# Row sums of image B's attention by transfer, and a reordered front, in a conv-attention kernel

## The chip, the cores and the metric

One core of one Trainium2 chip runs the whole program. The metric is the device time in microseconds (us) of one execution; less is better. PE is the matrix engine, PEld its weight loads, DVE the vector engine, ACT the scalar engine, POOL the GpSimd engine. SP is the engine that here only issues transfers. All data are fp32.

## The reference

The input is eight images of 512 channels and 32x32 pixels. Each is group-normed and sent through a block whose output is added back to the input:

```python
t = cbs(x, cv1_w, cv1_bn, 0)              # 1x1 conv, batch norm, SiLU
ys = [t[:, :C], t[:, C:]]                 # C = 256
for i in range(2):
    yi = ys[-1]
    z = cbs(yi, m_cv1_w[i], m_cv1_bn[i], 1)               # 3x3 conv
    z = bot_attention(z, m_qkv_w[i], m_rw[i], m_rh[i])    # 4 heads of 64, 1024 pixels
    z = silu(bn(conv2d(z, m_cv2_w[i], 0)))
    ys.append(yi + z)
return cbs(concatenate(ys), cv2_w, cv2_bn, 0)
```

Attention divides by the row sums of the exponentials. They are the subject of the larger part of the change.

## The kernel before

**Staging.** A front (roughly the first 77 us) norms the first images, turns the 3x3 filters into transformed filters (`make_u`) and begins the first 1x1 convolutions (`cv1`). Then the loop over p = 0 to 3 takes a pair of images A = 2p and B = 2p + 1. For each of two blocks (n = 0 and 1) it runs a transformed 3x3 convolution over both images (`conv3x3`), then per image a projection to q, k and v, the attention (`attention_fast`) and a 1x1 convolution (`m2`). Work of the next pair (its norm and its `cv1`, called `nxt`) is threaded in between. For p = 1 and 2 `nxt` is a Strassen scheme (`strassen_cv1`, seven products of four matmuls). For p = 0 it is direct, eight matmuls per output chunk. For p = 3 there is no next pair and the gap is filled with halves of the last convolution (`cv2_part`).

**Order.** Each engine executes its instructions in order. The order on each engine follows the program text, adjusted by a scheduler when the kernel is built. `tc.issue_after(x)` puts what its block traces on x's engine behind x on that engine.

**Attention.** Four groups (channel half c, pixel half) of eight key chunks. PE makes logits (line 1032), ACT the exponentials (line 1036), DVE adds them up into `acc` (lines 1050 and 1052), and PE multiplies by v (line 1066). The av product leaves PSUM at lines 1073 and 1074. The reciprocals of the row sums reach the output z by two ways:

- By transfer, for all groups but one: `sums` (line 1076) sums over partitions with four matmuls of 256 columns, ACT copies, SP stores the row to DRAM, `spread` (line 1122) reads it back as 128x8, inverts it on DVE (line 1126), writes it out and reads it back broadcast over 64 partitions each (line 1130). `scale` (line 1138) multiplies z by it. That is four transfers in sequence.
- At once (`at_once=True`), for the last group of image A in block 0 of p = 0 and of image B in block 0 of every p: `last_sums` (line 1093) makes the sums with an all-ones matrix of 64 columns, so that they already stand on all partitions. ACT copies them (line 1107), DVE adds the two halves (line 1182), inverts the full 128x512 (line 1183) and scales. Five further transfers (lines 1109 and 1114) and one add (line 1115) only keep the sums for a later range check.

**Behind image B's attention in block 0** (lines 2074 to 2096). PE runs the row sums, then `nxt.begin` (or the first `cv2_part`), then `m2` of image B, then the rest of `nxt`, then the next `conv3x3`. DVE makes the input tiles of that convolution: `tiles_in(Y2[0], ..., [0])` for image A, which has been ready for long, and `tiles_in(Y2[1], ...)` for image B, which needs all of m2's output. Each index i of `tiles_steps` has five pieces, from `w_ba`, `w_ec` or `w_g` (lines 554 to 561) to `v_in` (lines 595 to 603). Parts for image A with i = 1 and 2 come from DRAM (line 2084). In `conv3x3` PE writes `c_ps` (line 648), ACT copies a part (`c_m`, line 653), and DVE does the inverse transform (`c_t`, line 667, to z, line 699). PSUM has three buffers of this size.

**Front.** `make_u` treats one chunk (n, oc, k) in three steps i = 2, 0, 1. DVE does sums and differences (lines 430 to 435), ACT two copies per step (u0 and u5, lines 428 and 429), POOL the stores. Steps 0 and 1 first overwrite `mid` (lines 409 to 417). `chunk` is (0, 1, 0), `other` is (0, 1, 1). `behind_u` (line 1613) is called by `group_norm_part` while it applies the second image's norm on ACT (line 782) and puts work between these parts.

Of the kernel before, what the change touches and what calls it, by code (L numbers as in the profile page):

```python
# [47 lines left out]
ALU = mybir.AluOpType  # L48
# [13 lines left out]
def kernel(  # L62
# [325 lines left out]

    halves_of_u, copied_u, copies_behind, chunk_made = [], [None], [None], [None]

# [8 lines left out]

    def make_u(n, oc, k, area, full=None, new=u_new_late, stores=None, summed=True):  # L400

# [3 lines left out]
        for i in (2, 0, 1):  # L405
# [19 lines left out]
            if i < 2:  # L425
                yield last
            with tc.issue_after(copies_behind[0].ins) if copies_behind[0] else nullcontext():
                nc.scalar.activation(u0, c0, AF.Identity, scale=0.25)
                copied_u[0] = nc.scalar.copy(u5, c2)
            tt(u2, c0, c2, ALU.add)  # L430
            tt(u1, u2, c1, ALU.add)
            yield tt(u2, u2, c1, ALU.subtract)
            stt(u4, c2, 4.0, c0, ALU.mult, ALU.add)
# [52 lines left out]
    def stages(act, small, ps_big, ps_av, n_pt):  # L486
# [9 lines left out]
        silu_in, last_product, silued, last_exp, m2_silu, conv_product, cleared = [], [None], [None], [None], [None], [None], [None]  # L496
        shift_made, applied_x, projected = [None], [None], [None]

# [510 lines left out]
        def attention_fast(qkv, ao, at, behind, at_once=False):  # L1009
# [112 lines left out]
            def spread(g, s_dram):  # L1122

                rs = act.tile([P, HALF], F32, tag="rs", name="rs", bufs=4)
                rc = small.tile([P, QP], F32, tag="rc", name="rc", bufs=2)
                nc.vector.reciprocal(rc, total(g, s_dram))
                r_dram = tc.dram_tile([2, HALF], F32, name=f"r_dram{at + g}")
                nc.sync.dma_start(r_dram.rearrange("h (i r) -> (h i) r", r=QP), rc)
                for hd in range(2):
                    nc.sync.dma_start(  # L1130
                        rs[hd * HD : (hd + 1) * HD, :], r_dram[hd : hd + 1, :].to_broadcast([HD, HALF])
                    )
                return rs
# [33 lines left out]
            if not at_once:  # L1167
                with tc.issue_after(evicted[0].ins):
                    scale(g - 1, rss.pop(g - 1))
                return SimpleNamespace(  # L1170
                    evicted=evicted[0],
                    sums=lambda: s_drams.update({g: sums(g)}),
                    spread=lambda: rss.update({g: spread(g, s_drams[g])}),
                    scale=lambda: scale(g, rss.pop(g)),
                )
# [73 lines left out]

        def cv1(w_of, xts, y0s, y1, ocs, begun={}):  # L1250

            for oc in ocs:
                ps, at = begun.get(oc, (None, 0))
                ps = cv1_products(w_of, xts, oc, range(at, NX), ps)
                for half in range(NH):
                    dst = y0s[half][:, oc, :] if oc < NM else inner(y1, oc - NM, half)
                    silu(planes(dst), natural(ps[:, half, :]), bn_cv1 + oc)
# [114 lines left out]
        def strassen_cv1(w, xts, y0s, y1, t_tile):  # L1372
# [5 lines left out]

            def product(w, rhs, ps=None):
                onto = ps is not None  # L1380
                if not onto:
                    ps = ps_big.tile([P, 2, HALF], F32, tag="big", name="x_ps")
                for o in range(2):
                    for c in range(2):
                        nc.tensor.matmul(  # L1385
                            ps[:, o, :], w[:, c, ts(o, P)], rhs[c], start=(c == 0 and not onto), stop=(c == 1),
                            skip_group_check=onto,
                        )
                return ps
# [12 lines left out]
            y0_2, y1_1, y1_2 = y0s[1], side(y1, 0), side(y1, 1)  # L1402

            def begin():
                kept["ps"] = product(w["11"], b11)
                kept["m1"] = to(spare("p3"), kept["ps"])

# [5 lines left out]

            def sums(after=None):
                kept["t"] = t1, t2, t3, t4 = [t_tile() for _ in range(4)]
                for c in range(2):
                    tt(t1[:, c], b12[c], b11[c], ALU.subtract)
                with tc.issue_after(after.ins) if after else nullcontext():
                    for c in range(2):
                        tt(t2[:, c], b22[c], t1[:, c], ALU.subtract)  # L1420
                        tt(t3[:, c], b22[c], b12[c], ALU.subtract)
                        tt(t4[:, c], t2[:, c], b21[c], ALU.subtract)

# [24 lines left out]

            return begin, go_on, sums, rest, add_y0, add_y1, finish

        def cv2_part(w_of, rhs_of, oc, tag):

            ps = cv2_products(w_of, rhs_of, oc, range(2 * NM), ends=(0, 2 * NM - 1))
            part = act.tile([P, HW], F32, tag=tag, name="part")
            for half in range(NH):
                nc.scalar.copy(part[:, ts(half, HALF)], ps[:, half, :])
            return part
# [155 lines left out]
    def behind_u(c):  # L1613
        if c == 2:
            copies_behind[0] = s.applied_x[0]
            with tc.issue_after(s.added_eps[0].ins):
                next(chunk)
            with tc.issue_after(s.shift_made[0].ins):
                chunk_made[0] = next(chunk)
            with tc.issue_after(s.applied_x[0].ins), tc.issue_after(copied_u[0].ins):  # L1620
                s.cv1(w1_of, xs, y0s, Y1[0], Y_ORDER[2:3], begun)
            return s.silued[0]
        return copied_u[0] if c == 1 else s.silued[0] if c else None

# [63 lines left out]
    chunk = make_u(0, 1, 0, areas[0, 1, 0], new=u_new_early, stores=kept_back)  # L1688
    other = make_u(0, 1, 1, areas[0, 1, 1], new=u_new_early, stores=kept_back)
    with tc.issue_after(made.ins):  # L1690
# [9 lines left out]
    with tc.issue_after(copied_u[0].ins):  # L1700
        s.cv1(w1_of, xs, y0s, Y1[0], Y_ORDER[1:2], begun)
    first = begin(Y_ORDER[3], [0, 1])
    with tc.issue_after(made.ins), tc.issue_after(first.ins):
# [4 lines left out]
    with tc.issue_after(made.ins), tc.issue_after(s.silued[0].ins), tc.issue_after(first.ins):  # L1708
        multiplied, read, applied, powered = next(norm)
    copies_behind[0] = None  # L1710
    with tc.issue_after(powered.ins):
        put_stores(kept_back)
    with tc.issue_after(chunk_made[0].ins), tc.issue_after(powered.ins):
        for made in other:
            put_stores(kept_back)
# [84 lines left out]
    for p in range(NP):  # L1800
# [23 lines left out]
        def next_cv1(which, xts, y1, b):  # L1824
# [17 lines left out]
            if direct:  # L1842
                one = lambda oc: s.cv1(w_of, xts, y0s, y1, [oc])
                return SimpleNamespace(
                    begin=lambda: one(0), go_on=lambda: one(1), sums=nothing,
                    rest=lambda i: one(i) if i > 1 else None, adds=nothing, adds2=nothing, finish=nothing,
                    keep=lambda: keep_y(b, y0s, y1),
                )
            f = s.strassen_cv1(take_blocks("sw", None, which, SW_NAMES), xts, y0s, y1, t_qk)
            names = ("begin", "go_on", "sums", "rest", "adds", "adds2", "finish")  # L1850
            return SimpleNamespace(keep=lambda: keep_y(b, y0s, y1), **dict(zip(names, f)))
# [202 lines left out]
        def step_part():  # L2054
            next(parts_at, None)

        at_keys = ((1, 3), (2, 1), (2, 3), 3, (3, 2)) if more else [(g, at) if at else g for g in range(NG) for at in range(1, 4)]
        behind = hooks(NORM_B, {0: 1, 1: 1, 4: 1}, {key: step_part for key in at_keys}) | {
            NG + 1: begin_cv1(1, Y1[1], ia + 3)
        }  # L2060
        if not more:
# [10 lines left out]

            behind[NG + 1] = parts_of([0])
        end = s.attention_fast(qkv, z[:, :, 1], at_of(ib, 0), behind, at_once=True)
        while step_u():
            pass
        for _ in parts_at:
            pass
        if more:
            nxt.sums(end.scaled)  # L2080
        vs = v_units()
        for i in range(1, NI):
            for cp in range(3):
                nc.sync.dma_start(vs[i, cp][:, :, 0], v_dram[i][cp])
        with tc.issue_after(end.scaled.ins):
            s.tiles_in(Y2[0], putter(vs, 0), [0])
        last = s.m2(0, z[:, :, 1], Y1[1], lambda oc, half: inner(Y2[1], oc, half))
        if more:
            nxt.go_on()
            for i in range(4):  # L2090
                nxt.rest(i)
        else:
            parts_of([1, 2, 3])()
        with tc.issue_after(last.ins):
            s.tiles_in(Y2[1], putter(vs, 1))
            end.check()


        feed(units(1) + sqs(1, 0))
        z = new_z()  # L2100
# [214 lines left out]
```

## Time and profile before

| | |
|---|---|
| runs | median 2258.35 us of 3 (2257.54 to 2260.1) |
| the profiled execution | 2258.25 us, span of its instructions 2256.7 us |
| mean granted PE clock over the span | 0.998 of full speed |
| chain of work that ended last | PE 77%, DVE 15%, issue 3%, ACT 2%, DMA 1% |
| reciprocal at once, line 1183 | 5 times, 3353 ns each |
| reciprocal by transfer, line 1126 | 59 times, about 196 ns each |
| row-sum matmuls at once, line 1100 | from 308.1 to the next product at 309.1 us (p = 0) |
| image B's attention in block 0, last av matmul ends | 307.5, 860.4, 1409.9, 1932.7 us for p = 0 to 3 |

Engine shares are averages over stages with different limits, and a matmul's end is modelled. A busy engine is therefore read stretch by stretch, and an idle one by what ended its idle time.

### The profile page before, as it was taken

How to read it: one execution, taken by the hardware profiler on the slowest of the kernel's cores; microseconds unless marked ns; L12 is line 12 of the kernel's file. 1: busy time of each engine (PE TensorE's matmuls, PEld its weight loads, DVE VectorE, ACT ScalarE, POOL GpSimd, SP SyncE). 2: the span in 40 equal slices, each digit the busy share in tenths (PEclk: the TensorE clock that was granted, in tenths of full speed). 3: DMA queues.
4: the chain of work that ended last, by engine and by line, in shares of the span. 5: the costliest groups of instructions: out<-in, count | busy, mean ns of one | idle time of the engine just before them, and what ended most of it. 6: DMA issues, size and time to landing. Idle time of an engine off the chain costs nothing.

```text
span 2256.7 us, 40558 instructions
## 1 busy us (share of the span) xinstructions
PE 2209.9 (98%) x16346; PEld 1078.5 (48%) x16346; DVE 1746.1 (77%) x2679; ACT 1104.3 (49%) x1367; POOL 225.0 (10%) x417
## 2 busy tenths in 40 slices
PE   7999999999999999999999999999999999999998
PEld 3553438343474444633447343654345733473443
DVE  7988898878578689877947868987784868887652
ACT  7554553644225765455324667355622455335533
POOL 3322210000220000000021000000012000000001
PEclk9999999999999999999999999999999999999999
DMA  9854537221581324521257150532137611261214
GB/s 274 292 174 137 202 103 264 91 94 49 139 274 49 113 89 132 182 64 65 66 154 260 30 176 31 194 113 84 46 82 177 222 49 50 64 204 35 67 45 112
DMA packets 134580, 284.60 MB, mean 126 GB/s; under 512 B 34320, under 2 KB 61948, under 8 KB 133360
## 3 DMA queue, kind: packets, MB, share of 16 engines
q1 hardware_dynamic: 102480, 196.31, 26.6%
q0 software_dynamic: 31904, 85.61, 13.2%
q8 instruction: 131, 2.15, 0.4%
q14 instruction: 65, 0.53, 0.1%
HBM read 213.83 MB, written 68.03 MB: 125 GB/s over the span
## 4 chain that ended last, share of the span: by engine, by line
PE 77%; DVE 15%; issue 3%; ACT 2%; DMA 1%; POOL 0%; SPq 0%; DVEq 0%; ACTq 0%; POOLq 0%
PE av_ps L1066 16%; PE l_ps L1032 15%; PE c L1285 9%; PE c_new L1285 6%; PE ps L518 6%; PE p_ps L911 6%; PE c_ps L648 5%; PE m_ps L1265 5%; PE x_ps L1385 4%; PE p_ps L917 3%; DVE acc L1052 2%; PE s_ps L1083 1%; DVE c_e L675 1%; DVE c_t L668 1%; DMA u<-u_new 1%
## 5 line engine op out<-in xcount | busy, mean ns | idle before, releaser
L1036 ACT ACTIVATE pt<-l_ps 128x1024 f32<-128x1024 f32 x512 | 495.5, 1023 | 339.7 <-PE l_ps L1032 228.2
L1052 DVE TENSOR_TENSOR acc<-acc,pt 128x1024 f32<-128x1024 f32 x384 | 469.8, 1223 | 60.1 <-ACT pt L1036 35.1
L1032 PE MATMUL l_ps<-q,kr 64*64 64x512 f32 x4096 | 486.4, 590 | 2.3 <-ACT pt L1036 1.5
L1066 PE MATMUL av_ps<-pt,vT 64*64 64x512 f32 x4096 | 485.9, 591 | 1.8 <-DVE z L1074 1.5
L1032 PEld LDWEIGHTS l_ps<-q,kr 64*64 64x64 f32 x4096 | 158.0, 133 | 272.1 <-issue 251.0
L1066 PEld LDWEIGHTS av_ps<-pt,vT 64*64 64x64 f32 x4096 | 155.1, 133 | 275.3 <-issue 250.7
L648 PEld LDWEIGHTS c_ps<-v_in,u 128*64 128x64 f32 x4320 | 235.7, 137 | 5.4 <-issue 5.3
L648 PE MATMUL c_ps<-v_in,u 128*64 128x128 f32 x4320 | 237.6, 273 | 0.0
L1265 PE MATMUL m_ps<-z,m_sb 128*128 128x512 f32 x256 | 112.5, 592 | 0.0
L653 ACT COPY c_m<-c_ps 128x512 f32<-128x512 f32 x48 | 28.1, 585 | 172.2 <-PE c_ps L648 123.2
L911 PE MATMUL p_ps<-t_z,sq 128*128 128x512 f32 x224 | 107.0, 595 | 0.0
L1074 DVE TENSOR_TENSOR z<-av_ps,z 128x512 f32<-128x512 f32 x64 | 44.1, 688 | 72.2 <-ACT z L1073 72.1
L490 ACT ACTIVATE t<-m_ps,bh,sh 128x512 f32<-128x512 f32 x64 | 46.3, 773 | 87.2 <-PE m_ps L1265 87.2
L911 PE MATMUL p_ps<-z,sq 128*128 128x512 f32 x168 | 80.1, 604 | 4.9 <-ACT z L490 4.9
L1050 DVE TENSOR_TENSOR acc<-pt 128x1024 f32<-128x1024 f32 x64 | 77.8, 1216 | 6.7 <-ACT pt L1036 6.7
L1335 POOL DMA_DIRECT2D c_out<-in_x_dram x56 | 50.4, 973 | 280.4 <-ACT c_out L490 277.0
L1265 PEld LDWEIGHTS m_ps<-z,m_sb 128*128 128x128 f32 x256 | 48.3, 190 | 58.8 <-issue 56.7
L490 ACT ACTIVATE c_out<-cz,bh,sh 128x512 f32<-128x512 f32 x14 | 16.7, 1296 | 91.2 <-DVE cz L1362 91.2
L1138 DVE TENSOR_TENSOR z<-z,rs 128x512 f32<-128x512 f32 x64 | 43.9, 687 | 21.4 <-DMA rs<-r_dram 20.9
L490 ACT ACTIVATE z<-z,bh,sh 128x512 f32<-128x512 f32 x64 | 47.7, 804 | 17.2 <-DVE z L699 16.5
L1385 PE MATMUL x_ps<-t_x,sw 128*128 128x512 f32 x128 | 55.9, 592 | 0.0
L911 PEld LDWEIGHTS p_ps<-t_z,sq 128*128 128x128 f32 x224 | 38.9, 191 | 33.1 <-issue 33.1
(311 smaller groups left out, 3179.9 us busy)
## 6 DMA issues: line engine op xcount, KB each, us to landing
u<-u SPq DMA_DIRECT2D x135, 512.0 KB
sq<-sq SPq DMA_DIRECT2D x42, 384.0 KB
rs<-r_dram SPq DMA_DIRECT2D x118, 128.0 KB
x<-in_x_dram SPq DMA_DIRECT2D x28, 512.0 KB
r_in<-r SPq DMA_DIRECT2D x28, 512.0 KB
y_in<-y SPq DMA_DIRECT2D x28, 512.0 KB
c_out<-in_x_dram POOLq DMA_DIRECT2D x56, 256.0 KB, 5.3
out_dram<-c_out POOLq DMA_DIRECT2D x56, 256.0 KB, 4.1
```

Source lines behind the costliest of these rows:

```text
L490: silued[0] = nc.scalar.activation(dst, src, AF.Silu, scale=sh[:, k : k + 1], bias=bh[:, k : k + 1])
L518: last_product[0] = nc.tensor.matmul(ps[:, half, :], w_of(k), rhs_of(k, half), start=(k == begin), stop=(k == end))
L648: conv_product[0] = nc.tensor.matmul(to[o], us[cp][:, k, row, c, o], rhs, start=(k == 0), stop=(k == NM - 1),)
L911: nc.tensor.matmul(ps[:, o, :], w[:, o, :], rhs, start=not onto, stop=True, skip_group_check=onto)
L1032: nc.tensor.matmul(ps[kh * HD : (kh + 1) * HD, hd, :], kr[r, c, o : o + HD], q[r, c, ts(half, HALF)], start=True, stop=True,)
L1036: last_exp[0] = exp = nc.scalar.activation(pt, ps, AF.Exp, scale=SCALE)
L1050: return nc.vector.tensor_tensor(accs[g], pt[0], pt[1], ALU.add)
L1052: ins = nc.vector.tensor_tensor(accs[g], accs[g], pt[i], ALU.add)
L1066: nc.tensor.matmul(avs[g][hd * HD : (hd + 1) * HD, kh, :], vT[r, j, o : o + HD], pt[i][r, hd, :], start=(j == 0), stop=(j == NJ - 1),)
L1265: nc.tensor.matmul(pss[half][:, oc, :], m2_sb[:, n, k, ts(oc, P)], ao[:, k, ts(half, HALF)], start=(k == 0), stop=(k == NM - 1),)
L1285: nc.tensor.matmul(ps[:, o, :], w[:, k, ts(o, P)], rhs[part][:, c], start=(k == 0 and not onto), stop=(k == KB - 1), skip_group_check=onto,)
L1385: nc.tensor.matmul(ps[:, o, :], w[:, c, ts(o, P)], rhs[c], start=(c == 0 and not onto), stop=(c == 1), skip_group_check=onto,)
```

## The change

Image B's attention in block 0 is called without `at_once`, so its last group goes by transfer. The code behind it is reordered: half of the first product of `nxt` stands before the row sums and the other half behind; the next product (`go_on`, or a second `cv2_part`) moves from behind m2 to before it; the sums for `nxt`, `spread` and pieces of image A's tiles are placed in a written order; the loads of line 2084 and of the next filters go behind the broadcast. The range check needs no transfer of its own any more. In the front, `other` makes the copies of its steps 2 and 0 on DVE; `cv1` of chunk `Y_ORDER[2]` gets its last products earlier and its two halves' SiLU apart; the order of steps of `chunk` around the norm is rewritten. The function calls threaded through (`cv1` with `halves`, `product` with `outs`, `cv2_part` with `begun`) serve this.

```diff
-            with tc.issue_after(copies_behind[0].ins) if copies_behind[0] else nullcontext():
-                nc.scalar.activation(u0, c0, AF.Identity, scale=0.25)
-                copied_u[0] = nc.scalar.copy(u5, c2)
+            if i not in by_dve:
+                with tc.issue_after(copies_behind[0].ins) if copies_behind[0] else nullcontext():
+                    nc.scalar.activation(u0, c0, AF.Identity, scale=0.25)
+                    copied_u[0] = nc.scalar.copy(u5, c2)
...
-            yield tt(u2, u2, c1, ALU.subtract)
+            last = tt(u2, u2, c1, ALU.subtract)
+            if i in by_dve:
+                nc.vector.tensor_scalar(u0, c0, 0.25, None, ALU.mult)
+                last = nc.vector.tensor_copy(u5, c2)
+            yield last
...
+            def begin_half():
+                kept["ps"] = product(w["11"], b11, outs=[0])
+
+            def begin_rest():
+                product(w["11"], b11, kept["ps"], [1], onto=False)
+                kept["m1"] = to(spare("p3"), kept["ps"])
...
-            def sums(after=None):
+            def sums(after=None, middle=None):
                 kept["t"] = t1, t2, t3, t4 = [t_tile() for _ in range(4)]
-                for c in range(2):
-                    tt(t1[:, c], b12[c], b11[c], ALU.subtract)
                 with tc.issue_after(after.ins) if after else nullcontext():
                     for c in range(2):
+                        tt(t1[:, c], b12[c], b11[c], ALU.subtract)
+                for c in range(2):
+                    with tc.issue_after(after.ins) if after else nullcontext():
                         tt(t2[:, c], b22[c], t1[:, c], ALU.subtract)
                         tt(t3[:, c], b22[c], b12[c], ALU.subtract)
-                        tt(t4[:, c], t2[:, c], b21[c], ALU.subtract)
+                        last = tt(t4[:, c], t2[:, c], b21[c], ALU.subtract)
+                    if c == 0 and middle:
+                        with tc.issue_after(last.ins):
+                            after = middle()
+                return last
...
     def behind_u(c):
         if c == 2:
-            copies_behind[0] = s.applied_x[0]
-            with tc.issue_after(s.added_eps[0].ins):
-                next(chunk)
-            with tc.issue_after(s.shift_made[0].ins):
-                chunk_made[0] = next(chunk)
-            with tc.issue_after(s.applied_x[0].ins), tc.issue_after(copied_u[0].ins):
-                s.cv1(w1_of, xs, y0s, Y1[0], Y_ORDER[2:3], begun)
-            return s.silued[0]
-        return copied_u[0] if c == 1 else s.silued[0] if c else None
+            with tc.issue_after(s.applied_x[0].ins):
+                s.cv1(w1_of, xs, y0s, Y1[0], Y_ORDER[2:3], begun, [1])
+        return None if c == 1 else s.silued[0]
...
-    other = make_u(0, 1, 1, areas[0, 1, 1], new=u_new_early, stores=kept_back)
+    other = make_u(0, 1, 1, areas[0, 1, 1], new=u_new_early, stores=kept_back, by_dve=(2, 0))
...
+    begin(Y_ORDER[2], range(NX // 2, NX))
+    with tc.issue_after(s.silued[0].ins):
+        s.cv1(w1_of, xs, y0s, Y1[0], Y_ORDER[2:3], begun, [0])
...
+    copies_behind[0] = applied
+    with tc.issue_after(read.ins):
+        next(chunk)
+    with tc.issue_after(s.shift_made[0].ins):
+        made = next(chunk)
     copies_behind[0] = None
     with tc.issue_after(powered.ins):
         put_stores(kept_back)
-    with tc.issue_after(chunk_made[0].ins), tc.issue_after(powered.ins):
+    with tc.issue_after(made.ins), tc.issue_after(powered.ins):
         for made in other:
             put_stores(kept_back)
...
-        end = s.attention_fast(qkv, z[:, :, 1], at_of(ib, 0), behind, at_once=True)
-        while step_u():
-            pass
-        for _ in parts_at:
-            pass
+        end = s.attention_fast(qkv, z[:, :, 1], at_of(ib, 0), behind)
         if more:
-            nxt.sums(end.scaled)
+            nxt = next_cv1(1, xs, Y1[1], ia + 3)
+            nxt.begin_half()
+        else:
+            begun_part = s.cv2_products(w2_top, rhs_direct, 0, range(NM), ends=(0, 2 * NM - 1))
+        end.sums()
+        if more:
+            nxt.begin_rest()
+        else:
+            parts[0] = s.cv2_part(w2_top, rhs_direct, 0, "p1", (NM, begun_part))
+        last = end.added
+        with tc.issue_after(last.ins):
+            while step_u():
+                pass
+            for last_part in parts_at:
+                last = last_part or last
+        if more:
+            nxt.go_on()
+        else:
+            parts_of([1])()
...
         vs = v_units()
-        for i in range(1, NI):
-            for cp in range(3):
-                nc.sync.dma_start(vs[i, cp][:, :, 0], v_dram[i][cp])
-        with tc.issue_after(end.scaled.ins):
-            s.tiles_in(Y2[0], putter(vs, 0), [0])
+        pieces = s.tiles_steps(Y2[0], putter(vs, 0), [0])
+        if more and not direct:
+            last = nxt.sums(last, spread)
+        for at in range(2 if more and not direct else 5):
+            with tc.issue_after(last.ins):
+                last = next(pieces)
+                if at == 2:
+                    last = spread()
+        with tc.issue_after(last.ins):
+            scaled = end.scale()
+        with tc.issue_after(s.spread_out[0].ins):
+            for i in range(1, NI):
+                for cp in range(3):
+                    nc.sync.dma_start(vs[i, cp][:, :, 0], v_dram[i][cp])
+        with tc.issue_after(scaled.ins):
+            for last in pieces:
+                pass
         last = s.m2(0, z[:, :, 1], Y1[1], lambda oc, half: inner(Y2[1], oc, half))
         if more:
-            nxt.go_on()
             for i in range(4):
                 nxt.rest(i)
         else:
-            parts_of([1, 2, 3])()
+            parts_of([2, 3])()
```

## The prediction

> **What bounds the kernel now.** I read the page first, then PE's waits, then windows and timelines around image B's attention in block 0 and in the front. In the page row (busy us, share, instructions) and the waits (total us, times, longest):
>
> ```profile
> PE 2209.9 (98%) x16346; PEld 1078.5 (48%) x16346; DVE 1746.1 (77%) x2679; ACT 1104.3 (49%) x1367; POOL 225.0 (10%) x417
> ...
> PE s_ps L1100 <- DVE acc L1052: 6.2, 4, 2.4
> ...
> PE c_ps L648 <- DVE v_in L602: 4.9, 3, 2.3
> ```
>
> PE is the bound on average, and two of its waits sit where the change works: before the at-once row sums (6.2 us in all, four sites) and at the first convolution (4.9 us). The average hides a second bound. The windows over the next convolution, for p = 0 to 3 (PE, PEld, DVE, ACT, POOL busy, then the clock):
>
> ```profile
> 348.00:381.90 33.90, 33.45 (x528) 30.93 (x523) 32.92 (x71) 9.44 (x14) 2.33 (x3) 1.00 0.88 322
> 863.20:933.70 70.50, 69.00 (x674) 48.58 (x674) 69.78 (x137) 28.11 (x31) 3.25 (x11) 1.00 0.61 207
> 1412.70:1483.00 70.30, 69.00 (x674) 48.57 (x674) 69.64 (x138) 28.12 (x31) 3.25 (x11) 1.00 0.62 207
> 1976.70:2010.60 33.90, 33.44 (x527) 30.92 (x523) 32.92 (x71) 9.44 (x14) 1.28 (x1) 1.00 0.79 267
> ```
>
> DVE is busy 32.9 of 33.9 us and 69.8 of 70.5 us: as full as PE. After these stretches PE waits (0.45 to 0.87 us) for the z that DVE has just made. So the end of each site is set by **DVE's chain**: end of m2, adds into ypad, three tiles of image B, inverse transform. DVE's own timeline at p = 0 (start, length):
>
> ```profile
> 325.82 1.23 DVE L554 SCALAR_TENSOR_TENSOR w_ba<-ypad 128x1024 f32<-128x1024 f32 x1
> ...
> 344.55 0.42 DVE L603 TENSOR_TENSOR v_in<-w_ab 128x256 f32<-128x256 f32 x1
> 348.07 0.69 DVE L667 TENSOR_TENSOR c_t<-c_ps,c_m 128x512 f32<-128x512 f32 x1 [3.10 <-ACT c_m L653]
> ```
>
> The three tiles take 19.15 us (325.82 to 344.97); only at p = 0 and 3 does DVE then stand idle (3.10 and 3.56 us) until the convolution delivers. At p = 1 and 2 it never does.
>
> **Part 1: the row sums, PE's side.** From PE's timeline, a product of four 128x128x512 matmuls takes 3.43 us, eight take 6.86 (322.96 to 329.82), m2 6.87 (316.09 to 322.96). The at-once sums take 1.02 (308.10 to 309.12), those by transfer 0.56 (296.43 to 296.99). The half product in front covers `acc`'s lateness: 1.72 us at p = 1 and 2 against waits of 1.59, 3.43 at p = 0 and 3 against 0.58 and 2.43. Saved on PE: 6.2 + 4 x 0.46 = 8.0 us. At p = 3 there is more:
>
> ```profile
> 1935.09 1.09 PE L1100 MATMUL s_ps<-acc,ones 64*64 64x512 f32 x8 [2.43 <-DVE acc L1052]
> 1936.11 5.40 PE L518 MATMUL ps<-y_in,w 128*128 128x512 f32 x8
> ...
> 1936.10:1939.50 3.40, 3.40 (x8) 1.41 (x5) 2.77 (x3) 1.07 (x2) 0.22 (x2) 0.52 0.95 292
> ```
>
> Behind the wait the granted clock is 0.52, and the eight records take 5.23 us to the next start instead of 3.43: 1.8 us more. [...] PE's saving is thus up to 9.8 us, if PE were the bound.
>
> **Part 2: DVE's side.** Removed per site: line 1182 (0.6 net), 1183 (3.35), 1115 (0.12); added, 0.2 for line 1126: 3.9 us net. But the next late thing is m2, because `go_on` now stands before it. Counting from the last av matmul (T):
> - p = 0: 3.43 + 0.56 + 3.43 + 6.86 + 6.87 = T + 21.2 = 328.7, before 322.96.
> - p = 1, 2: 1.72 + 0.56 + 1.72 + 6.86 + 6.87 = T + 17.7; p = 1: 878.1, before 873.38.
> - p = 3: as p = 0, T + 21.2 = 1953.9, before 1951.64.
>
> From m2's end to the start of image B's tiles: 2.3 us when DVE is free (1951.64 to 1954.05 less the dropped 0.12). Then 19.15 us.
> - **p = 0**: tiles end at 328.7 + 2.3 + 19.15 = 350.15; DVE's first `c_t` before was 348.07. Later by 2.1, less 0.7 of idle in the second step that closes: **+1.4**.
> - **p = 1, 2**: tiles start at 880.4, before 881.69. Nothing idle behind: **-1.2 each**. The 3.9 us are mostly turned into idle time, waiting for m2.
> - **p = 3**: tiles end at 1975.35, `c_t` before at 1976.76: -1.4, and the same 0.7: **-2.1**.
>
> PE's convolution starts earlier at each site (p = 0: about 342.5 instead of 343.65) and so is no limit; its saving beyond DVE's is lost to PSUM waits.
>
> **Part 3: the wait that is added.** m2's matmuls on the first pixel half don't read the last group, nor does the first of the second half. They cover 3.43 + 0.86 us. From the start of the sums' matmuls the scale must be done within 0.56 + 1.72 + 6.86 + 4.29 = 13.4 us (p = 1, 2) or 15.1 (p = 0, 3). The nearest rows are the other last groups, which already go by transfer. Eleven of them take 11.8 to 13.4 us from matmul to scale, plus 0.69. The slowest starts its matmuls at 1850.8; SP's queue, then DVE:
>
> ```profile
> 1852.26 0.52 SPq L1090 DMA_DIRECT2D s_dram<-s_row  x1
> 1853.89 0.31 SPq L1119 DMA_DIRECT2D sums_all<-s_dram  x1
> ...
> 1855.93 0.32 SPq L1128 DMA_DIRECT2D r_dram<-rc  x1
> 1859.17 1.11 SPq L1130 DMA_DIRECT2D rs<-r_dram  x2
> ...
> 1855.70 0.20 DVE L1126 RECIPROCAL rc<-sums_all 128x8 f32<-128x8 f32 x1 [3.07 <-DMA sums_all<-s_dram]
> ```
>
> `r_dram` took 3.2 us there beside a weight load. At the present site the third group's reciprocal at 858.05 was followed by its scale at 864.06: 6.0 us, not 8.5. In the changed order the 256 KB loads of line 2084 stand behind the broadcast and don't crowd it. I take 4.9 + 6.0 + 0.7 = 11.6 us: hidden, cost 0. By the worst row, 14.1, it costs 0.7 us at p = 1 and 2. Behind the waiting reciprocal on DVE stand three sums of `nxt` and two tile pieces at p = 1, 2 (1.8 + 2.4 us), two pieces at p = 0, 3; all fit before m2's output comes. SP issues five transfers for five (lines 1090, 1119, 1128 and twice 1130 instead of four times 1109 and 1114), each behind its own wait; the filter loads that stand behind them aren't needed for some 20 us. POOL's order is untouched here.
>
> **Part 4: the front.** DVE's timeline:
>
> ```profile
> 50.44 0.43 DVE L435 SCALAR_TENSOR_TENSOR u_new<-taps,u_new 128x256 f32<-128x256 f32 x1
> 54.35 0.56 DVE L415 SCALAR_TENSOR_TENSOR taps<-taps 128x384 f32<-128x384 f32 x1 [3.48 <-ACT u_new L429]
> ...
> 58.15 1.22 DVE L554 SCALAR_TENSOR_TENSOR w_ba<-ypad 128x1024 f32<-128x1024 f32 x1
> ```
>
> `mid` can't be overwritten until ACT has copied from it, and ACT does so behind the norm at 53.62. With these copies on DVE the 3.48 us go. Four copies are added there. By the nearest row (128x256, one per 0.335 us) they cost 1.34; two fall at 34 to 36 us, ahead of 0.89 us of idle at 40.7, so 0.67 counts. [...] I take the row. What is late next: POOL's memset before line 592 (61.09), queued behind stores that wait for ACT's step-1 copies. ACT loses four copies (1.2 us) and SiLU of half a chunk moves into its gap of 2.35 us before 45.35, so these come 1.4 to 3 us earlier. Between 2.0 and 3.3 I take **-2.6**; PE's own front gap of 1.16 us at 49.9 closes beside it, so PE is done about 74.2 and DVE's tile about 74.7. The following waits of 1.07 and 1.59 us are DVE's and shift with it.
>
> **Sum.** -2.6 + 1.4 - 1.2 - 1.2 - 2.1 = -5.7 us. The profiled execution took 2258.25 (span 2256.7 and 1.55 around it), within 0.1 of the median: **2252.6 us**.
>
> **Rivals.**
> - **The round trip is late (slower).** The place is m2's second half; beyond 13.4 us (15.1 at p = 0, 3) each us delays m2, and DVE's full chain, by one. The first attention's first group took 18.8 us (167.3 to 186.1, in DMA traffic), and at 1923.6 SP held the second transfer 4.6 us instead of 1.6 behind a tile load that waited for its store. At 18.8: 2 x 5.4 + 2 x 3.7 = 18.2, net +12.5: 2270.8. It decides the sign from about 16 us. Against it: those loads are moved behind. Chance 0.18.
> - **DVE's chain takes all back at image B** (m2 later by what DVE saves, order on DVE a little worse): only the front remains, 2255.7. For it: p = 0 loses already. Chance 0.15.
> - **PE is the bound after all**: 9.8 + about 3 in the front, 2245.5. Against it: the full DVE windows. Chance 0.06.
>
> My forecast has 0.61. A measurement here tells 0.2% (4.5 us) from no change; the threshold of 2253.8 is close, so of the 0.61 I count 0.49 faster and 0.12 the same. Faster 0.55, same 0.28, slower 0.17. The ends of the terms (front -1 to -3.5, p = 0 +0.5 to +2.5, p = 1, 2 -2 to +0.7 each, p = 3 -3.5 to 0) span 2246.5 to 2262; 2247 to 2260.5 leaves about 0.2 out.
>
> **What would show it.** No wait at the row sums; clock 1.0 behind p = 3's; DVE idle a few us before the last ypad adds at p = 1, 2; `c_t` first at about 350 less the front's gain at p = 0; no wait of m2 for `scale`; line 415 without its idle time. Wrong, if m2 waits for line 1138, or if DVE isn't the last to end in the convolutions.

## The result and the profile after

The changed kernel takes 2253.81 us (median of 11 executions, 2252.25 to 2255.87), the kernel before 2258.79 us beside it (11 executions). The ratio is 0.9979, 95% interval 0.9970 to 0.9988, that is 2.7 to 6.8 us less. The profiled execution's span is 2250.8 us against 2256.7, so 5.9 us less. The forecast sum was 5.7.

The page of the changed kernel, busy us by engine, and then PE's waits (total us, times, longest):

```profile
PE 2209.8 (98%) x16346; PEld 1079.1 (48%) x16346; DVE 1728.8 (77%) x2675; ACT 1101.3 (49%) x1359; POOL 225.1 (10%) x417
...
PE c_ps L653 <- DVE v_in L607: 3.1, 2, 1.9
PE c_ps L653 <- issue: 2.5, 4, 0.6
PE p_ps L922 <- DVE c_t L673: 2.5, 4, 0.6
```

PE does the same work. DVE has 17.3 us less, most of it four reciprocals. PE's 6.2 us of waits for `acc` at the row sums are gone, but each site now has a PE wait of 0.63 us inside the convolution ("issue": the profile names nothing that ended it) and one of about 0.63 us for DVE at its end; before had the second only at p = 1 and 2 (0.63 and 0.43 us). Part of what PE saves goes into these waits. Windows inside the same convolutions and inverse transforms, p = 0 to 3 (PE, PEld, DVE, ACT, POOL busy, then the clock):

```profile
345.00:376.00 31.00, 30.37 (x496) 27.75 (x490) 30.83 (x63) 6.76 (x10) 2.01 (x3) 1.00 0.93 345
894.00:927.00 33.00, 32.01 (x522) 29.20 (x518) 32.81 (x66) 7.67 (x12) 1.28 (x1) 1.00 0.83 289
1442.00:1476.00 34.00, 32.74 (x535) 29.96 (x531) 33.60 (x69) 7.96 (x12) 1.28 (x1) 1.00 0.82 282
1968.00:2001.00 33.00, 31.82 (x518) 29.01 (x514) 32.83 (x67) 7.76 (x12) 1.27 (x1) 1.00 0.80 276
```

DVE is full there. Ahead of it stands idle time. DVE's timeline at p = 1 (start, length, idle before and its cause in brackets):

```profile
865.26 0.20 DVE L1131 RECIPROCAL rc<-sums_all 128x8 f32<-128x8 f32 x1 [0.75 <-DMA sums_all<-s_dram]
...
871.03 0.69 DVE L1143 TENSOR_TENSOR z<-z,rs 128x512 f32<-128x512 f32 x1 [1.26 <-DMA rs<-r_dram]
...
877.51 1.36 DVE L1278 TENSOR_TENSOR ypad<-t,ypad 128x512 f32<-128x512 f32 x2 [0.77 <-ACT t L495]
878.90 1.22 DVE L559 SCALAR_TENSOR_TENSOR w_ba<-ypad 128x1024 f32<-128x1024 f32 x1
```

DVE waits 0.77 us for m2's SiLU before the last two adds, then begins image B's tiles. The transfer came in time. On PE, m2 runs without a wait for `scale` at all four sites; at p = 1:

```profile
869.63 7.03 PE L1270 MATMUL m_ps<-z,m_sb 128*128 128x512 f32 x16
```

To see each part I cut the traces at two marks. A **site** runs from the end of the last av record of image B's attention in block 0 to the first logits record of the next attention. All times below are such differences; "front" is the end of that last av record at p = 0.

| kernel | front | p = 0 | p = 1 | p = 2 | p = 3 | sum of sites |
|---|---|---|---|---|---|---|
| before | 307.5 | 87.07 | 86.00 | 85.73 | 90.63 | 349.4 |
| after | 304.7 | 88.47 | 85.04 | 85.04 | 88.46 | 347.0 |
| difference | -2.9 | +1.40 | -0.96 | -0.69 | -2.17 | -2.4 |

The stretches between the sites give the remaining 0.6 us; among all traces they differ by up to 2.5 us, and by 1.2 us between two traces of the kernel before.

### The profile page after: what moved, and what is told of

Its sections match the earlier page's. It is cut to its first block, busy times and chain, and to the rows that moved or that the text cites. A ratio compares the mean times of both kernels' runs of the same rounds, so it can differ in the third digit from the quotient of the medians.

```text
span 2250.8 us, 40563 instructions
## 1 busy us (share of the span) xinstructions
PE 2209.8 (98%) x16346; PEld 1079.1 (48%) x16346; DVE 1728.8 (77%) x2675; ACT 1101.3 (49%) x1359; POOL 225.1 (10%) x417
## 3 DMA queue, kind: packets, MB, share of 16 engines
q8 instruction: 131, 2.15, 0.4%
## 4 chain that ended last, share of the span: by engine, by line
PE 82%; DVE 11%; issue 3%; ACT 2%; DMA 1%; POOL 0%; SPq 0%; DVEq 0%; POOLq 0%; ACTq 0%
PE av_ps L1071 17%; PE l_ps L1037 16%; PE c L1290 9%; PE c_ps L653 7%; PE c_new L1290 6%; PE p_ps L916 6%; PE ps L523 5%; PE m_ps L1270 5%; PE x_ps L1390 4%; PE p_ps L922 3%; DVE acc L1057 1%; PE s_ps L1088 1%; PE p_ps L886 1%; DVE c_e L680 1%; ACT ypad L495 0%
## 5 line engine op out<-in xcount | busy, mean ns | idle before, releaser
L922 PEld LDWEIGHTS p_ps<-sq,z 128*128 128x128 f32 x336 | 42.9, 191 | 26.3 <-issue 12.5
```

Source lines behind the costliest of these rows:

```text
L922: nc.tensor.matmul(v[:, ts(j, P)], rhs[:, ts(j, P)], w[:, 2, :], start=j == 0 and not onto, stop=True, skip_group_check=True,)
```

## The experiments

Medians are of 4 to 11 executions, but for the last row. The ratio is to the kernel before on the same chip, with its 95% interval. The last three columns come from the trace.

| run | median us | ratio | span | front | sum of sites |
|---|---|---|---|---|---|
| front only | 2254.3 | 0.9989 (0.9980 to 0.9998) | 2251.0 | 304.2 | 347.0 |
| sites only | 2256.5 | 0.9993 (0.9984 to 1.0002) | 2255.9 | 307.3 | 347.0 |
| DVE longer | 2259.0 | 1.0005 (0.9995 to 1.0014) | 2258.0 | 305.0 | 352.3 |
| PE longer | 2254.8 | 0.9990 (0.9981 to 0.9999) | 2251.8 | 304.6 | 347.7 |
| half behind | 2247.7 | 0.9955 (0.9941 to 0.9968) | 2246.2 | 304.3 | 340.7 |
| all behind | 2250.0 | 0.9970 (0.9958 to 0.9982) | 2248.6 | 305.6 | 343.0 |
| order alone | 2261.0 | 1.0016 (1.0007 to 1.0025) | 2259.2 | 304.9 | 354.0 |
| ACT copies, first trace | 2255.3 | 0.9992 (0.9983 to 1.0002) | 2252.8 | 305.8 | 347.1 |
| ACT copies, second trace | 2255.3 | 0.9991 (0.9981 to 1.0000) | 2252.9 | 306.0 | 347.0 |
| scale first | 2247.7 | 0.9950 (0.9933 to 0.9967) | 2247.0 | 305.8 | 340.8 |
| loads last | 2259.7 | 1.0009 (1.0000 to 1.0019) | 2258.4 | 305.1 | 352.2 |
| before, second trace | 2256.2 (one) | | 2254.7 | 307.2 | 346.6 |

**The change in two parts.** Front only is the kernel before with the pieces of the diff that belong to the front (`by_dve`, the new order of `chunk`, `behind_u`, the halves of `cv1`). Sites only has the rest.

> The front of the changed kernel (two of other's copy pairs on VectorE, the new order of its chunks) with image B's second stage as before. The theory: the front's part is separate from the four sites. It is worth 2.9 us up to the end of image B's attention of block 0 (that end came at 307.5 us before and at 304.7 us in the changed kernel), and nothing more is gained or lost behind it: about 2.9 us under before, a little above the changed kernel's 2253.8. Rival: the sites take the front's gain back or double it (in the changed kernel the four sites and the stretches between them sum to -3.0 us, which could hold a gain that only an earlier front allows); then this one ends anywhere else, at 0 to -1 us or at -4 us and more.

> The four second-stage attentions of image B as in the changed kernel (sums handed over by a transfer, PE's work ahead of m2, no reciprocal of 128x512), the front as before. The theory: the sites alone are worth +1.4, -1.0, -0.7 and -2.2 us (the differences found between the two traces from the end of image B's attention to the next attention's first logits), with small shifts between them about -3 us. Rival: the sites give nothing without the front, 0 us.

In the front column both parts come out almost as expected: the front is worth 2.4 us as the mean of nine traces with it and with its copies on DVE (304.2 to 305.8, mean 304.9) against three without it (307.2 to 307.5, mean 307.3). But the sites brought a surprise. The front-only kernel has the old sites, and their sum is 347.0, not 349.4. The whole difference is p = 3, 88.35 instead of 90.63 us. With these old sites the sum is the same as with the new ones, so in the traces the rival of sites only (0 us) holds, not its theory. Its ratio leaves both open (1.6 us less, from 3.6 less to 0.5 more). PE's timeline of the front-only kernel at p = 3:

```profile
1931.25 1.09 PE L1105 MATMUL s_ps<-acc,ones 64*64 64x512 f32 x8 [1.87 <-DVE acc L1057]
1932.27 3.70 PE L523 MATMUL ps<-y_in,w 128*128 128x512 f32 x8
```

Eight records take 3.70 us, not the 5.40 of the first trace of before. The clock stayed at 1.0.

**The low clock again.** The kernel before was traced a second time.

> The kernel before, for a second trace. In its first trace the granted clock was 0.5 for 3.4 us behind the row sums at p=3 (an idle time of PE of 2.43 us ahead of them), and the site took 90.63 us; in the front-only kernel, which has the same row sums, the idle time was 1.87 us, the clock stayed at 1.0, and the site took 88.35. Theory that the clock follows from the idle time at this place: the low clock is there again, and the site takes 90.6 us. Rival that it falls by chance on some executions: full clock, and the site takes about 88.4 us.

Full clock, 88.07 us. But the idle time is shorter too, 1.57 us, so this trace alone does not rule out that the clock follows from it; two equal idle times in the front do (last section). PE's timeline at p = 3, then a window of the same length and place as the one in the prediction, which showed 0.52:

```profile
1934.76 1.09 PE L1100 MATMUL s_ps<-acc,ones 64*64 64x512 f32 x8 [1.57 <-DVE acc L1052]
1935.78 3.70 PE L518 MATMUL ps<-y_in,w 128*128 128x512 f32 x8
```

The window:

```profile
1935.80:1939.20 3.40, 3.40 (x11) 1.60 (x9) 2.77 (x3) 1.07 (x2) 0.22 (x2) 1.00 0.90 272
```

The low clock at p = 3 does not come with the old row sums every time: of four traces with these sums (before twice, front only, order alone) one has it, the one with the longest idle time ahead. Of the ten traces with the new sums none has it there. The site of that one trace is 2.3 to 2.6 us longer than in front only and in the second trace of before: 1.7 us are its eight records (5.40 instead of 3.70), the rest is its longer wait (2.43 instead of 1.87 and 1.57). Against the other two with the old order, 88.07 and 88.35 us, the changed kernel's 88.46 at p = 3 is no gain at all.

A trace shows one execution, but the mean granted clock of each execution is on record, to three decimals. One stretch of 3.4 us at half clock lowers it by 0.0008 (3.4 x 0.5 / 2257). Of the 82 executions of before beside these experiments, 42 have 0.997 or less and take 2258.8 us on average; the other 40 have 0.998 or more and take 2256.6. At 0.997 or less are 1 of 11 of front only, 2 of 11 of sites only, and none of 11 of the changed kernel, which take 2253.8 on average. All 82 average 2257.7 us, 4.0 more than the changed kernel: 2.8 us at an equal clock of 0.998 or more, about what the front gives, and some 1.2 us that go with the clock. (The eleven of before beside the changed kernel average 2258.5; their clocks are not on record, and the 82 are from three chips.) Where in these executions the clock was low is not on record either. Whether it is the wait at the old row sums that the change spares them is therefore not shown.

**Which engine sets a site.** Two kernels add work behind m2 in the changed kernel, one on DVE, one on PE.

```diff
                 ba = row_tile("w_ba")
-                last = stt(ba, rows(1, 2), -4.0, rows(3, 2), ALU.mult, ALU.add)
+                for _ in range(1 + again):            # again = 1 for image B here
+                    last = stt(ba, rows(1, 2), -4.0, rows(3, 2), ALU.mult, ALU.add)
```

> The changed kernel with one more VectorE operation at each of the four sites, behind m2's adds and ahead of image B's input tiles: its first one (w_ba, 128x1024, 1.22 us) is done twice. Theory that VectorE's chain behind m2 sets each site's end: 4 x 1.22 = 4.9 us longer than the changed kernel, seen at each site as 1.2 us more from the end of the attention to the next attention's first logits. Theory that PE is the bound there: no change, within 1 us.

```diff
             for i in range(4):
-                nxt.rest(i)
+                nxt.rest(i, 1 if i == 2 else 0)       # two matmuls once more
```

> The changed kernel with more PE work at each of the four sites behind m2: two matmuls of 128x128 by 128x512 (four records of 0.43 us pitch, 1.72 us) are done once more in the third of the products that follow m2. Theory that VectorE's chain sets the site's end: PE's added 1.72 us fill its waits there (0.63 us inside the convolution, 0.63 and 0.87 us at its end), 0 to 1 us in all over the changed kernel. Theory that PE is the bound: 4 x 1.72 = 6.9 us longer.

DVE longer adds 1.31, 1.31, 1.31 and 1.32 us to the sites. PE longer adds 0.13, 0.33, 0.14 and 0.13. The extra operation on DVE's timeline at p = 1:

```profile
881.30 1.22 DVE L560 SCALAR_TENSOR_TENSOR w_ba<-ypad 128x1024 f32<-128x1024 f32 x1
882.45 0.68 DVE L564 TENSOR_TENSOR w_ec<-ypad 128x512 f32<-128x512 f32 x1
883.05 1.22 DVE L560 SCALAR_TENSOR_TENSOR w_ba<-ypad 128x1024 f32<-128x1024 f32 x1
```

And PE's timeline with the longer PE work:

```profile
892.48 31.66 PE L655 MATMUL c_ps<-v_in,u 128*64 128x128 f32 x576
...
928.02 1.13 PE L924 MATMUL p_ps<-sq,z 128*128 128x128 f32 x8 [0.26 <-DVE c_t L675]
```

The convolution starts 1.7 us later in its site and now runs without the pause of 0.63 us inside; the wait at its end has shrunk from 0.63 to 0.26. The added PE work fell into PE's waits. DVE's chain is the bound, and PE has about 1.5 us to give at each site (1.72 less the 0.13 to 0.33 that come through).

**The order without the transfer, the transfer without the order.** The sites combine two edits: the row sums by transfer, and a product of 6.88 us put ahead of m2. Order alone starts from the front-only kernel. All behind starts from the changed one and keeps the rest of its order:

```diff
# order alone
+        nxt.go_on()                                   # p = 3: parts_of([1])()
         last = s.m2(...)
-            nxt.go_on()
# all behind
-            nxt.go_on()
         ...
         last = s.m2(...)
+            nxt.go_on()
```

> The front-only kernel with the product of 6.88 us put ahead of m2 at the four sites: the new order without the transfer (sums of 64x512 and the reciprocal of 128x512 as before). Theory: VectorE's chain starts at m2's end, which comes 6.9 us later; in the front-only kernel the sites took 87.25, 85.70, 85.71 and 88.35 us, and with 66.9 us from m2's end to the next logits they come to 89.5, 87.0, 87.0 and 90.6 us: about 7 us over the front-only kernel. Rival (the end isn't tied to m2): within 1 us of the front-only kernel.

> The changed kernel with the whole product that it had put ahead of m2 (6.88 us of PE) back behind m2: the transfer of the sums without the new order. The scale ends 13.2 us (p=1, 2) and 14.7 to 15.3 us (p=0, 3) after the attention in the changed kernel, and m2's first matmul that reads the scaled part would now be due at 8.6 us (p=1, 2) and 12.05 us (p=0, 3). Theory: PE waits for the scale 4.6 us at p=1 and p=2 and about 3 us at p=0 and p=3; PE has about 2.1 us of waits at each site to take it from, so 2.5 us longer at p=1 and p=2 and 0.6 to 1.2 us at p=0 and p=3: about 7 us over the changed kernel. Rival: VectorE alone sets the site, PE's wait is absorbed, and since m2 ends earlier the time is under the changed kernel's by 4 us or more.

Order alone: 89.38, 86.97, 86.96, 90.73 us, 7.0 us more than front only, within 0.2 us of the expected length at each site. The transfer alone: 86.17, 85.33, 85.34, 86.16 us, 4.0 us less than front only. So the transfer with the rest of the order gains 4.0, the product ahead of m2 costs 7.0 by itself and 4.0 beside the transfer, and together the four sites gain nothing at full clock. My expectation for all behind was wrong in sign, and its rival held: I let PE stand idle until the scale. PE's timeline at p = 1 of that kernel:

```profile
862.24 1.02 PE L1270 MATMUL m_ps<-z,m_sb 128*128 128x512 f32 x2
864.05 3.70 PE L1270 MATMUL m_ps<-z,m_sb 128*128 128x512 f32 x8 [0.78 <-DVE z L1143]
867.59 6.26 PE L1390 MATMUL x_ps<-x,sw 128*128 128x512 f32 x14
873.68 2.74 PE L1270 MATMUL m_ps<-z,m_sb 128*128 128x512 f32 x6
```

The product's records stand between the two parts of m2. PE idles 0.78 us, not 4.6.

From m2's last record to the next logits it is 66.9 us at every site in after and in order alone, and 66.9 (p = 1, 2) and 67.2 us (p = 0, 3) in all behind and in half behind, which follows. So the time of m2's end is what is to be bought. In before and front only it was 71.5 to 72.8: there m2 was done early, and DVE's own backlog (p = 1, 2) or PE (p = 0, 3, where DVE stood idle 3.1 to 3.6 us) came later.

**Half of it behind.** Between the two: half of the product ahead of m2 and half behind.

```diff
-            nxt.go_on()
+            nxt.go_half()                             # product s4; p = 0, 3: first half of the k
         ...
         last = s.m2(...)
+            nxt.go_rest()                             # product 12; p = 0, 3: the other half
```

> The changed kernel with the second half of the product that it had put ahead of m2 (3.44 us of PE) back behind m2. In the changed kernel VectorE's last idle at each site is its wait for m2's silu: 3.62 and 2.07 us at p=0, 0.77 us at p=1, 1.26 us at p=2, 4.24 and 2.07 us at p=3. Theory (VectorE's chain behind m2's end sets the site, the transfer of the sums still lands in time): m2 ends 3.4 us earlier at p=0 and p=3 and some 2.3 us earlier at p=1 and p=2, where PE waits about 1.1 us for the scale; the sites get shorter by 2.1 us at p=0 and p=3 (as much as PE's waits there leave), 0.8 us at p=1 and 1.3 us at p=2, in all 6.2 us under the changed kernel. Rival: the transfer is exposed at once, PE's wait for the scale goes to the end of the sites, and the time is no less, or up to 3 us more, than the changed kernel's.

86.18, 84.19, 84.19, 86.16 us: 6.3 us less than the changed kernel. It is the best version found, 2247.7 us, 7 to 13 us under the kernel before. DVE's timeline at p = 1:

```profile
874.38 0.42 DVE L608 TENSOR_TENSOR v_in<-w_ab 128x256 f32<-128x256 f32 x1
874.90 1.36 DVE L1278 TENSOR_TENSOR ypad<-t,ypad 128x512 f32<-128x512 f32 x2
876.29 1.23 DVE L559 SCALAR_TENSOR_TENSOR w_ba<-ypad 128x1024 f32<-128x1024 f32 x1
```

The last adds follow image A's pieces with 0.1 us between: the wait of 0.77 us is gone. At p = 0 and 3 DVE still waits 2.9 us ahead of its last adds, but there PE has only one wait of about 0.45 us left.

**Two tries to go further.**

```diff
# scale first
-        last = s.m2(0, z[:, :, 1], Y1[1], ...)
+        last = s.m2(0, z[:, :, 1], Y1[1], ..., scaled)   # its adds behind scale
# loads last, in addition
-        with tc.issue_after(s.spread_out[0].ins):
+        with tc.issue_after(scaled.ins):
             for i in range(1, NI): ...                   # loads of v_in
```

> The half-behind kernel with m2's adds on VectorE ordered behind the scale. In the half-behind kernel m2's second half waits 2.6 us for the scale at p=1 and p=2, and there VectorE does two of m2's adds (868.89 to 870.17) ahead of the scale, though the broadcast was issued at 865.63 and such a broadcast was there 3.6 us after its issue in the changed kernel, so at about 869.2. Theory: the scale starts about 1 us earlier at p=1 and p=2, m2 ends 1 us earlier, and both sites get 1 us shorter; p=0 and p=3, where the scale already waits for the transfer, stay: 2 us under the half-behind kernel's 2247.7. Rival: the two adds only move behind the scale and VectorE's chain stays as long: 0 us, or the broadcast lands later than that and PE gains nothing.

> As the kernel with the scale first, and the six 256 KB loads of v_in wait for the scale instead of for the issue of the broadcast. Theory: these loads run beside the broadcast's two transfers of 128 KB and stretch them from about 2.5 to 3.4 us; without them the scale comes about 1 us earlier at all four sites, and the sites get up to 1 us shorter each, 2 to 4 us in all. Rival: the loads don't matter to the broadcast: no change within 0.5 us in m2's end at any site.

Scale first moved nothing (sites within 0.02 us). At p = 1 the scale now waits for the transfer itself, and PE's order, not the scale, holds m2's second part; the 2.6 us that the expectation took for a wait are six records of the product:

```profile
870.09 0.69 DVE L1143 TENSOR_TENSOR z<-z,rs 128x512 f32<-128x512 f32 x1 [0.68 <-DMA rs<-r_dram]
...
870.19 2.74 PE L1391 MATMUL x_ps<-x,sw 128*128 128x512 f32 x6
872.76 2.74 PE L1270 MATMUL m_ps<-z,m_sb 128*128 128x512 f32 x6
```

Loads last did the opposite of its name, so its question, whether the loads stretch the broadcast, is left open. The edit does not make the loads wait: `issue_after` orders the queue of the engine of its argument, `scaled` is DVE's, and the loads are SP's. Taken from behind the broadcast, they came to stand earlier in SP's queue. SP's queue, DVE and PE at p = 2:

```profile
1412.32 7.16 SPq L2143 DMA_DIRECT2D v_in<-v  x5
1419.53 0.54 SPq L1095 DMA_DIRECT2D s_dram<-s_row  x1
...
1423.57 0.20 DVE L1131 RECIPROCAL rc<-sums_all 128x8 f32<-128x8 f32 x1 [5.80 <-DMA sums_all<-s_dram]
...
1429.94 4.25 PE L1270 MATMUL m_ps<-z,m_sb 128*128 128x512 f32 x6 [3.46 <-DVE z L1143]
```

Five loads hold the store of the sums back until 1419.53, though the attention had ended at 1411.8; DVE waits 5.80 us, PE 3.46 us, and then the clock drops to 0.50 (six records in 4.25 us instead of 2.74). The sites take 2.4, 3.8, 5.1 and 0.0 us more than with the scale first; 1.5 of the 5.1 us are the low clock. This is the prediction's slower rival, made by accident: it is the price of loads in the wrong place of SP's queue.

**What in the front makes the gain.** The changed kernel with all copies back on ACT, the new order kept:

```diff
-    other = make_u(..., stores=kept_back, by_dve=(2, 0))
+    other = make_u(..., stores=kept_back)
```

> The changed kernel with the two copies of each of the two chunks of the front back on ScalarE, the new order of the front kept. Theory: the front's gain of 2.9 us comes from VectorE no longer waiting for these copies (before, it stood 3.48 us ahead of the third chunk's first operation); the wait returns, and the end of image B's attention of block 0 comes about 2.5 us later than in the changed kernel, near 307 us. Rival: the gain comes from the new order of the chunks; then within 0.5 us of 304.6 us.

> A second look at the kernel with the front's copies on ScalarE and the new order. In nine traces with the changed front the first tile operation of the front (w_ba) starts between 54.88 and 56.42 us, mean 55.50; in three with the front of before between 57.82 and 58.15, mean 57.95; in the first look at this kernel at 56.19. Theory that the copies on VectorE are worth about 0.9 us beside the order: again near 56.4, above the mean of the nine by 0.5 or more. Rival that the order alone makes the gain and the copies nothing: anywhere from 54.9 to 56.4, with equal chance on either side of 55.5.

DVE's timeline in the front, the changed kernel first:

```profile
46.82 0.28 DVE L435 TENSOR_SCALAR u_new<-taps 128x256 f32<-128x256 f32 x1
47.02 0.42 DVE L432 TENSOR_TENSOR u_new<-u_new,taps 128x256 f32<-128x256 f32 x1
...
50.13 0.42 DVE L438 SCALAR_TENSOR_TENSOR u_new<-taps 128x256 f32<-128x256 f32 x1 [2.15 <-DMA u<-u_new]
...
51.51 0.56 DVE L415 SCALAR_TENSOR_TENSOR taps<-taps 128x384 f32<-128x384 f32 x1
```

Then the first trace with the copies on ACT:

```profile
50.95 0.42 DVE L438 SCALAR_TENSOR_TENSOR u_new<-taps 128x256 f32<-128x256 f32 x1 [1.30 <-DMA u<-u_new]
...
52.39 0.56 DVE L415 SCALAR_TENSOR_TENSOR taps<-taps 128x384 f32<-128x384 f32 x1
```

Line 415, which waited 3.48 us for ACT's copies in before, waits no longer for them here though they are on ACT (0.88 us in the second trace). In both kernels DVE waits for a store that has to leave the `u_new` buffer (2.15 us; 1.75 and 1.30; 2.27). The first tile starts at 56.19 and 55.92 us, against a mean of 55.50 with the copies on DVE and 57.95 in before. So about 1.9 of the 2.4 us there come from the order. The copies' 0.6 us lie within the spread of the nine traces at the tile. At the end of the attention both traces (305.84 and 306.02 us) are above all nine, by 1.0 us over their mean, so neither theory nor rival of the first expectation met; 0.42 us over the mean at the tile is under the 0.5 that the second asked for. What the copies are worth, between 0 and 1 us, stays open.

## Why the prediction was right, and where it was not

- **What bounds the sites.** Right. DVE's chain behind m2 sets them (1.31 us for 1.22 us of DVE, 0.13 to 0.33 for 1.72 us of PE).
- **Row sums, PE's side.** The waits went as said, and PE's 8 us were not worth anything, as said. The clock term of this part (1.8 us) fell: it took a row of a single execution for the price of the old sums, and one of four traces with these sums pays it.
- **p = 0: +1.4.** Measured +1.40; in the second trace of before the site is again 87.07. The step (m2 later, the tiles behind it, DVE's idle times of 3.10 and 0.69 us closed) was right. Image B's tiles start 5.5 us later where the sum had 5.2, and DVE makes up 0.3 us more; that these two cancel is luck.
- **p = 1 and 2: -1.2 each.** The mechanism was right, the size too large: -0.96 and -0.69, and -0.68 for both against the second trace of before. The term that was mis-sized is m2's end: 18.13 us after the attention by its last record, which is modelled 0.16 us past the next start, so 17.97, where the sum had 17.7. The prediction's own numbers (880.4 against 881.69) give -1.3, not -1.2. DVE's wait ahead of the last adds is 0.77 and 1.26 us, not "a few us"; another 2.0 and 1.5 us stand ahead of the reciprocal and the scale. Besides, p = 2 was already 0.27 us shorter than p = 1 in the first trace of before, and the sum used p = 1 for both.
- **p = 3: -2.1.** The number met (-2.17), but by luck. 2.3 to 2.6 us of the difference are the longer wait and the low clock of one trace. Against 88.07 and 88.35 us the change is +0.4 and +0.1, like p = 0 with less to lose. This is the step of the prediction that failed: m2's end and the first `c_t` before (1951.64 and 1976.76) were those of an execution with low clock, taken for those of the kernel. With +0.3 in its place the sum is -3.3.
- **The sum: -5.7.** That 5.0 us were measured is in part luck too. At equal clock it is 2.8 us. Of the rest, some 1.2 us go with a clock that is often lower in executions of before; the prediction has that only through its row at p = 3. The ends of its terms, added up from 2258.25, are 2247.8 and 2261.2, not 2246.5 and 2262.
- **The added wait: 0.** Right. From the sums' matmul to the scale's start it took 11.1, 10.6, 10.2 and 10.5 us, plus 0.69 for the scale; 10.9 plus 0.7 were taken. Where the queue is badly ordered the rival's price is real (up to 5.1 us at a site, 1.5 of it low clock).
- **The front: -2.6.** Measured -2.9 in this pair of traces, -2.4 in the mean of all. The cause was half wrong. The idle time of line 415 went with the order more than with the copies, and what came late next was not POOL's memset but a `u_new` buffer's store (2.15 us). No run shows the 2.0 and 3.3 us that the -2.6 was taken between; the runs showed the 2.9 and 2.4 in their place. For a copy's cost I took the row (0.335 us); the copies start 0.20 us before the next operation. While POOL issued seven stores from 44.01 to 47.78 us, two copies started at 46.82 and 47.36 without a wait.
- **The rival "DVE's chain takes all back at image B".** It describes the sites best: their sum is 347.0 us in front only and in after. At full clock, what remains of the change is its front. Its 2255.7 us are 1.9 above the measured time; what goes with the clock is not in them.

The expected gain at the sites did not get lost in the transfer. DVE lost some 4 us of work at each site (1745.5 us busy in front only, 1728.8 in after), and the order gave that back as idle time ahead of m2's end, because 6.88 us of product were put ahead of m2 where half would cover the transfer.

## What to carry to other kernels

Work put in front of a step to cover a wait should be as long as the wait and no longer: here, where DVE behind that step sets the end, 3.44 us less of it (half behind against the changed kernel) made the sites 0.85 to 2.30 us shorter. To see which engine that is, add a known piece of work to each in turn. A term of a forecast that rests on a clock event in one trace should be held against a second trace and against the clocks of other executions first.

## What the hardware showed unexpectedly

The granted clock falls to 0.5 for about 3.4 us after some idle times of PE and not after others of the same length. At p = 2 of loads last the windows of 1 us from 1429 to 1433 have 0.70, 0.50, 0.50 and 0.59, together 3.4 us at half clock. In the front, PE waits for the first convolution's input in every trace. The changed kernel there had 1.93 us of it, and this window behind it:

```profile
75.60:78.70 3.10, 3.10 (x33) 3.10 (x31) 3.00 (x9) 0.00 (x0) 0.91 (x2) 0.50 1.01 407
```

Over the 14 traces of this place: after waits of 1.48 and 1.64 us never; after eight waits of 1.93 to 2.29 us five times; after four of 2.94 to 3.42 us always. Before has 2.26 us in both its traces, once with and once without. What decides between the two was not shown. In the front the event seems to cost little: among the nine kernels with the changed front the attention of p = 0 ends at 304.2 to 305.1 us without it (four) and at 304.6 to 305.8 with it (five), means 304.7 and 305.1. The five include the two longest waits, so less than these 0.4 us may be the clock's. At p = 3 of before it cost 1.7 us (5.40 instead of 3.70), at p = 2 of loads last 1.5 (4.25 instead of 2.74).
